# Softmax weights of later rows transposed on VectorE from blocks regrouped through DRAM, instead of on TensorE

## The chip, the cores and the metric

The kernel runs on one core of a Trainium2 chip. A core has a TensorE (PE) for matrix products, with the weight loads shown on their own as PEld; a VectorE (DVE), a ScalarE (ACT) and a GpSimd (POOL) for elementwise work; and SyncE (SP), which here only issues transfers. The engines run side by side and wait for each other through semaphores; each works through its own instructions in order. The metric is the time of one execution on the device in microseconds (us). All data is 32-bit floating point (f32).

## The reference

A block of cross-attention to a small bank of context rows, a mixture of three experts with soft routing, and a gate. B = 8 rows, T = 512 tokens, H = 256 channels, P = 64 context rows, E = 3 experts with RH = 512 hidden units.

```python
nx = _layer_norm(x, ln_gamma, ln_beta)
q = nx @ Wq
k = prototype_bank @ Wk
v = prototype_bank @ Wv
scores = jnp.einsum('bth,bph->btp', q, k) * H ** (-0.5)
weights = jax.nn.softmax(scores, axis=-1)
evidence = jnp.einsum('btp,bph->bth', weights, v)
anchor = jnp.broadcast_to(global_anchor[:, None, :], nx.shape)
combined = jnp.concatenate([nx, evidence, anchor], axis=-1)
router_probs = jax.nn.softmax(combined @ router_W + router_b, axis=-1)
h = jax.nn.silu(jnp.einsum('btc,ecr->bter', combined, e_w1) + e_b1)
expert_out = jnp.einsum('bter,erh->bteh', h, e_w2) + e_b2
routed = jnp.sum(expert_out * router_probs[..., None], axis=-2)
g = jax.nn.sigmoid(jax.nn.silu(combined @ gate_w1 + gate_b1) @ gate_w2 + gate_b2)
return x + g * (routed @ out_w + out_b)
```

## The kernel before

**Tiling.** The eight rows go in four pairs, j = 0 to 3. A pair's two rows are treated as a 2x2 block matrix, and the products are done with seven block products instead of eight; this is why differences of tiles are formed everywhere. Activations are held with channels on the 128 partitions and the 512 tokens along the free dimension (tiles of 128x512), the state in which TensorE wants them as the moving operand.

**Softmax weights.** `scores` computes the scores with *tokens* on the partitions: tile w of a pair is 128 partitions x 4 token groups x 2 rows x 64 context rows. `softmax` normalizes one row of the pair in it (L555, L556). The products of `evidence` need the same numbers the other way round: tile wT, 128 partitions (2 rows x 64 context rows) x 512 tokens. `transpose_w` makes it: four TensorE transposes of 128x128 into a PSUM bank (tile pt_w, L564) and a copy on ScalarE (L567). `evidence` multiplies it with vw, the value rows already multiplied by the first-layer weights (`value_weights`, L631, copied by L638, with a difference of two parts on VectorE at L645).

**Order.** The order on every engine is the order of the program: the lists `within` and `between` in the main loop put the small steps of a pair at named points of the large products. A pair runs `gate_layer`, three times `expert_layer`, then `outputs`. While `outputs` of pair j runs its second-layer products (12 matmul instructions for each 128x512 result, from L656), the steps in `between` prepare pair j + 1: scores, softmax, the transposes, the differences T on GpSimd (`combine_x`, L521), the value weights and the router. So there are three such blocks; in the profile they lie near 105 to 158, 213 to 266 and 321 to 374 us.

In `outputs` the points concerned come in this order: P2 (scores and softmax of the second row, differences of x), products, one output finished, P7 (`transpose_w`, value weights of expert 0, router logits), products, one output finished, P3 (value weights of expert 1, the router's exponentials), products, the last output finished, P4 (`router` for both rows). An output is finished by `finish`: L959 adds the PSUM result, L960 multiplies by the gate, L961 transposes the 32x32 blocks on VectorE, L962 adds x on GpSimd, and L951 stores it with four transfers on SP's queue. There are two buffers for yb, so every second output uses the same one.

`router` ends with the probabilities pr (L598, L600, L602 on VectorE, for each row). At the end of the next pair's gate products, `spread_probabilities` transposes the two pr on TensorE (tile pt_p, L615), copies them out (L616) and spreads them over all partitions through DRAM. Right behind pt_p come the first products of `evidence` with wT.

**Blocks through DRAM.** The normalized x of later pairs is already turned in this manner: `store_x` writes it to DRAM (xd, L497), `regroup_x` loads it back with `load_blocks` (L390) in such an order that each 32x32 block stands where its transpose belongs, and `transpose_blocks` (L509) lets VectorE transpose the blocks in place. All these transfers are on SP's queue. SP waits there for the write before it issues the loads.

PSUM has eight banks; small results take turns in the banks that `spares` names, through `misc`.

Of the kernel before, what the change touches and what calls it, by code (L numbers as in the profile page):

```python
# [8 lines left out]
F32 = mybir.dt.float32  # L9
# [7 lines left out]
def kernel(  # L17
# [50 lines left out]
    nc = tc.nc  # L68
    P = 128
    B, T, H = x.shape  # L70
    CT = context.shape[1]
    E, C3, RH = e_w1.shape
    KH = H // P
# [12 lines left out]
    dram = ctx.enter_context(tc.tile_pool(name="dram", bufs=2, space=bass.MemoryType.DRAM))  # L86
# [3 lines left out]
    work = ctx.enter_context(tc.tile_pool(name="work", bufs=2))  # L90
# [33 lines left out]
    def load_x(b):  # L124
        x_sb[b] = xpool.tile([P, NT, H], F32, tag="x", name=f"x_{b}")
        nc.sync.dma_start(x_sb[b], x[b].rearrange("(t p) d -> p t d", p=P))
# [5 lines left out]
    def rows_of(w):  # L132
        return w.rearrange("(k p) n -> p k n", p=P)
# [249 lines left out]
    def load_blocks(dst, src):  # L383

        for k in range(KH):
            for i in range(P // TB):
                lo = k * P + i * TB
                nc.sync.dma_start(  # L390
                    dst[i * TB : (i + 1) * TB, k, :].rearrange("r (j c) -> r j c", c=TB),
                    src[:, lo : lo + TB].rearrange("(j r) c -> r j c", r=TB),
                )
# [9 lines left out]
    def load_second(e):  # L403
        load_blocks(w2[e], e_w2[e])
# [44 lines left out]
    S = {}  # L449
# [102 lines left out]
    def softmax(b):  # L552
        w, sm = S["w", b // 2][:, :, b % 2, :], S.pop(("sm", b))
        rs = work.tile([P, NT], F32, tag="rs", name=f"rs_{b}")
        nc.vector.reciprocal(rs, sm)  # L555
        nc.vector.tensor_tensor(w, w, rs.unsqueeze(2).to_broadcast([P, NT, CT]), ALU.mult)  # L556

    def transpose_w(j):

        w = S["w", j]  # L560
        wT = work.tile([P, T], F32, tag="wT", name=f"wT_{j}", bufs=1)
        pt = misc(f"pt_w_{j}")
        for t in range(NT):
            nc.tensor.transpose(  # L564
                pt[:, t * P : (t + 1) * P], w[:, t, :, :].rearrange("p i c -> p (i c)"), ident
            )
        nc.scalar.copy(wT, pt)  # L567
        S["wT", j] = wT
# [487 lines left out]
    with tc.manual_schedule(engines=None):  # L1056
        ctx_rows = context.flatten_outer_dims().rearrange("(t p) d -> p t d", p=P)
        for d in range(2):
            half = slice(d * NX // 2, (d + 1) * NX // 2)
            nc.sync.dma_start(ctx_sb[:, half, :], ctx_rows[:, half, :])  # L1060
        nc.scalar.dma_start(wk_sb, rows_of(Wk))
        nc.scalar.dma_start(wv_sb, rows_of(Wv))
        load_x(0)
        nc.sync.dma_start(wq_sb, rows_of(Wq))
        load_x(1)
        for g in (E, 0):
            load_first(g)
            load_anchor(g)
        for g in (1, 2):
            load_first(g)  # L1070

        wake(7)
        context_transposes()
        project_keys()
        statistics(0, 0, NT)
        deviation(0, 0)
        normalize(0)
        project(wv_sb, ctxT, lambda m, ps: nc.scalar.copy(vT[:, m, :], ps), "v")
        small_transposes()
        wq_transposes()  # L1080
        transpose_x(0)
        router_anchor()
        statistics(1, 0, NT)
        deviation(0, 1)
        normalize(1)
        load_table(AF.Exp)
        project(wqT, kT, keep_m, "m")
        combine_weights(E)
        value_weights(0, E)
        spread_router_rows(0)  # L1090
        transpose_x(1)
        combine_x(0, nc.vector, (0, 1))
        scores(0)
        scores(1)
        load_table(AF.Silu)
        combine_weights(0)
        softmax(0)
        value_weights(0, 0, nc.vector.tensor_copy)
        anchor_rows(E)
        anchor_rows(0)  # L1100
        softmax(1)
        combine_x(0, nc.vector, (2, 3))
        combine_weights(1)
        combine_weights(2)
        late_scratch()
        load_anchor(1)
        load_anchor(2)
        nc.sync.dma_start(ow_sb, rows_of(out_w))
        nc.sync.dma_start(gw2_sb, rows_of(gate_w2))
        combine_gate()  # L1110
        load_second(0)

        for j in range(NP):


            within, between = {}, {}

            def put(where, n, step, *args):
                where.setdefault(n, []).append(lambda: step(*args))

            if j == 0:
                put(within, "gate", value_weights, 0, 1)
                put(within, (0, "A"), anchor_rows, 1)
                put(within, (0, "A"), router_logits, 0)
                put(within, (0, "A"), load_second, 1)
                put(within, (0, "B"), second_bias)
                put(within, (0, "B"), router_logits, 1)
                put(within, (0, "C"), transpose_second, 0)
                put(within, (0, "C"), anchor_columns, 1)
                put(within, (0, "C"), anchor_rows, 2)  # L1130
                for b in range(2):
                    put(within, (0, "C"), router_exp, b)
                    put(within, (0, "D"), router, b)
                put(within, (0, "C"), load_second, 2)
                put(within, (0, "D"), second_layer, 0)
                put(within, (0, "D"), spread_probabilities, 0)
                put(within, (0, "D"), combine_second, 0)
                put(within, (1, "A"), transpose_second, 1)
                put(within, (1, "B"), second_layer, 1)
                put(within, (1, "B"), combine_second, 1)  # L1140
                put(within, (1, "C"), transpose_second, 2)
                put(within, (1, "C"), anchor_columns, 2)
                put(within, (1, "D"), second_layer, 2)
                put(within, (1, "D"), combine_second, 2)
            if j:
                put(within, "gate end", spread_probabilities, j)
            put(within, (0, "C" if j == 0 else "B"), value_weights, j, 2)
            put(within, (1, "C"), load_x_blocks, 2 * j)
            put(within, (2, "A"), gate_differences, j)
            put(within, (2, "C"), load_x_blocks, 2 * j + 1)  # L1150
            if j + 1 < NP:
                b0, b1 = 2 * j + 2, 2 * j + 3
                put(within, "gate", load_x, b0)
                put(within, "gate", load_x, b1)
                put(within, (0, "A" if j else "D"), statistics, b0, 0, NT)
                put(within, (0, "C") if j else (1, "A"), statistics, b1, 0, NT)
                for i in range(2):
                    put(within, (1, "C"), deviation, j + 1, i)
                where = (1, "D") if j else (2, "B")
                put(within, where, normalize, b0)  # L1160
                put(within, where, store_x, b0)
                put(within, where, regroup_x, b0)
                put(within, (2, "C"), normalize, b1)
                put(within, (2, "C"), store_x, b1)
                put(between, "begin", transpose_blocks, b0)
                put(between, "gate", regroup_x, b1)
                put(between, "P1", scores, b0)
                put(between, "begin", value_weights, j + 1, E)
                put(between, "begin", spread_router_rows, j + 1)
                put(between, "P5", softmax, b0)  # L1170
                put(between, "P5", transpose_blocks, b1)
                put(between, "P6", router_logits, b0)
                put(between, "P2", scores, b1)
                put(between, "P2", softmax, b1)
                put(between, "P2", combine_x, j + 1, nc.gpsimd)
                put(between, "P7", transpose_w, j + 1)
                put(between, "P7", value_weights, j + 1, 0)
                put(between, "P7", router_logits, b1)
                put(between, "P3", value_weights, j + 1, 1)
                put(between, "P3", router_exp, b0)  # L1180
                put(between, "P3", router_exp, b1)
                put(between, "P4", router, b0)
                put(between, "P4", router, b1)
            gate_layer(j, within)
            for e in range(E):
                expert_layer(j, e, within)
            outputs(j, between)
# [34 lines left out]
```

## Time and profile before

| What | us |
|---|---|
| Median of 3 runs (475.64 to 476.08) | 476.01 |
| The profiled execution | 476.25 |
| Its span, first to last instruction | 474.5 |
| PE busy in the span | 469.6 |
| DVE busy in the span | 353.4 |
| L564, one of 16 transposes of w on PE | 0.273 |
| L567, one of 4 copies of wT on ACT | 0.587 |
| L509, one of 12 block transposes on DVE | 0.688 |

Times inside the profile count from the start of the span. The granted TensorE clock is 1.000. Busy time of PE is not time at its peak: matmuls overlap, and their ends are modelled, so starts of instructions are the safer measure. A line of the timeline gives start, duration, engine, line of the kernel, operation, output and input tiles, and in brackets the idle time of the engine ahead of it with what ended it.

### The profile page before, as it was taken

How to read it: one execution, taken by the hardware profiler on the slowest of the kernel's cores; microseconds unless marked ns; L12 is line 12 of the kernel's file. 1: busy time of each engine (PE TensorE's matmuls, PEld its weight loads, DVE VectorE, ACT ScalarE, POOL GpSimd, SP SyncE). 2: the span in 40 equal slices, each digit the busy share in tenths (PEclk: the TensorE clock that was granted, in tenths of full speed). 3: DMA queues.
4: the chain of work that ended last, by engine and by line, in shares of the span. 5: the costliest groups of instructions: out<-in, count | busy, mean ns of one | idle time of the engine just before them, and what ended most of it. 6: DMA issues, size and time to landing. Idle time of an engine off the chain costs nothing.

```text
span 474.5 us, 4652 instructions
## 1 busy us (share of the span) xinstructions
PE 469.6 (99%) x1451; PEld 225.1 (47%) x1451; DVE 353.4 (74%) x649; ACT 218.4 (46%) x391; POOL 78.2 (16%) x96
## 2 busy tenths in 40 slices
PE   9999999999999999999999999999999999999997
PEld 7654646435454444445454444445454444444454
DVE  2755766989989555889989565898989624697982
ACT  3555656557321546748320456758221365458000
POOL 5227032300062200000062200000042300000020
PEclk9999999999999999999999999999999999999999
DMA  8988330048311840342111750252011560000013
GB/s 285 369 126 159 59 134 1 0 103 104 33 22 22 168 145 0 78 101 44 17 24 22 155 155 2 62 115 46 18 22 22 83 185 0 1 0 1 0 22 67
DMA packets 118120, 35.27 MB, mean 74 GB/s; under 512 B 104732, under 2 KB 115088, under 8 KB 117584
## 3 DMA queue, kind: packets, MB, share of 16 engines
q1 hardware_dynamic: 114736, 27.02, 28.4%
q0 software_dynamic: 1472, 7.18, 4.7%
q10 hardware_dynamic: 1888, 0.79, 0.6%
q8 instruction: 11, 0.18, 0.2%
q14 instruction: 13, 0.11, 0.1%
HBM read 27.57 MB, written 7.40 MB: 74 GB/s over the span
## 4 chain that ended last, share of the span: by engine, by line
PE 94%; DVE 4%; issue 1%; ACT 0%; ACTq 0%
PE ps_u L656 42%; PE ps_z L656 18%; PE ps_y L656 15%; PE ps_vw L631 5%; PE ps_gu L656 3%; PE ps_s L531 3%; PE ps_w2o L416 2%; PE ps_gz L656 1%; DVE h L930 1%; PE ps_wake L255 1%; PE ps_k L310 1%; DVE h L739 1%; PE ps_gy L656 1%; PE ps_v L298 1%; PE ps_ar L354 0%
## 5 line engine op out<-in xcount | busy, mean ns | idle before, releaser
L739 DVE TENSOR_TENSOR h<-h,pb 128x512 f32<-128x512 f32 x96 | 61.9, 693 | 10.5 <-ACT h L689 10.5
L656 PE MATMUL ps_u<-h,w2o 128*128 128x512 f32 x144 | 63.9, 593 | 0.0
L656 PE MATMUL ps_u<-nxT,w 128*128 128x512 f32 x112 | 55.6, 607 | 0.0
L689 ACT ACTIVATE h<-h,abias 128x512 f32<-128x512 f32 x72 | 49.2, 718 | 8.7 <-DVE h L695 8.2
L656 PE MATMUL ps_z<-wT,vw 64*128 64x512 f32 x104 | 49.5, 605 | 0.0
L962 POOL TENSOR_TENSOR yb<-yb,xb 128x512 f32<-128x512 f32 x14 | 19.1, 1365 | 149.5 <-DVE yb L961 145.2
L656 PE MATMUL ps_z<-h,w2s 128*128 128x512 f32 x96 | 42.8, 595 | 0.2 <-DVE r L945 0.2
L698 ACT COPY h<-ps_u 128x512 f32<-128x512 f32 x48 | 28.0, 583 | 32.2 <-PE ps_u L656 31.9
L656 PEld LDWEIGHTS ps_u<-h,w2o 128*128 128x128 f32 x144 | 27.1, 190 | 31.3 <-issue 29.7
L695 DVE TENSOR_TENSOR h<-h,ps_y 128x512 f32<-128x512 f32 x24 | 16.4, 683 | 28.5 <-PE ps_y L656 28.5
L930 DVE TENSOR_TENSOR h<-h,h 128x1024 f32<-128x1024 f32 x24 | 34.3, 1483 | 0.0
L656 PEld LDWEIGHTS ps_u<-nxT,w 128*128 128x128 f32 x112 | 19.9, 189 | 29.7 <-issue 22.8
L689 ACT ACTIVATE h<-ps_u,abias 128x512 f32<-128x512 f32 x24 | 16.5, 687 | 30.4 <-PE ps_z L656 30.4
L656 PE MATMUL ps_y<-nxT,w 128*128 128x512 f32 x56 | 28.6, 592 | 0.0
L656 PE MATMUL ps_z<-T,ws 128*128 128x512 f32 x56 | 28.6, 592 | 0.0
L656 PEld LDWEIGHTS ps_z<-h,w2s 128*128 128x128 f32 x96 | 17.9, 190 | 22.1 <-issue 21.1
L656 PE MATMUL ps_u<-wT,vw 64*128 64x512 f32 x56 | 27.8, 611 | 0.0
L656 PE MATMUL ps_y<-wT,vw 64*128 64x512 f32 x56 | 27.0, 596 | 0.0
L631 PE MATMUL ps_vw<-w,vT 128*128 128x512 f32 (+1 forms) x64 | 26.9, 541 | 0.0
L656 PE MATMUL ps_u<-T,ws 128*128 128x512 f32 x56 | 26.7, 594 | 0.0
L656 PE MATMUL ps_u<-T,w 128*128 128x512 f32 x56 | 26.6, 592 | 0.0
L656 PE MATMUL ps_z<-nxT,ws 128*128 128x512 f32 x56 | 26.6, 592 | 0.0
(206 smaller groups left out, 771.8 us busy)
## 6 DMA issues: line engine op xcount, KB each, us to landing
pb<-pd POOLq DMA_DIRECT2D x4, 1536.0 KB, 7.1
x<-in_x_dram SPq DMA_DIRECT2D x8, 512.0 KB, 5.9
xb<-in_x_dram SPq DMA_DIRECT2D x64, 64.0 KB, 2.5
out_dram<-yb SPq DMA_DIRECT2D x56, 64.0 KB, 2.0
w<-in_L_xcond_e_w_dram SPq DMA_DIRECT2D x6, 512.0 KB, 9.3
xd<-x SPq DMA_DIRECT2D x6, 512.0 KB, 3.0
xg<-xd SPq DMA_DIRECT2D x48, 64.0 KB, 2.4
scr_wa<-in_L_xcond_e_w_dram SPq DMA_DIRECT2D x3, 512.0 KB, 4.7
```

The costliest lines, as they stand in the source:

```text
L255: nc.tensor.matmul(ps_wake[0][:, :P], zeros, zeros, start=True, stop=True)
L298: nc.tensor.matmul(ps, w_sb[:, k, m * P : (m + 1) * P], src[:, k, :], start=(k == 0), stop=(k == KH - 1))
L416: nc.tensor.matmul(ps[:, d * H : (d + 1) * H], w2T[:, k, (i + d) * P : (i + d + 1) * P], ow_sb[:, k, :], start=(k == 0), stop=(k == KH - 1),)
L531: nc.tensor.matmul(ps[:, t, :], nxT[:, k, t * P : (t + 1) * P], mr[:, k, b, :], start=(k == 0), stop=(k == KH - 1),)
L631: nc.tensor.matmul(ps, vT[:, k, j * 2 * CT : (j + 1) * 2 * CT], w1[:, KH + k, n0:n1], start=(k == 0), stop=(k == KH - 1),)
L656: nc.tensor.matmul(ps, lhsT, rhs, start=start, stop=True, skip_group_check=not start)
L689: nc.scalar.activation(h, h if src is None else src, AF.Silu, bias=abias[:, c, 2 * j + i : 2 * j + i + 1])
L695: nc.vector.tensor_tensor(h, h, part, ALU.add)
L698: nc.scalar.copy(chunk(n, i, d), part)
L739: nc.vector.tensor_tensor(h, h, S["pb", j][:, i, 2 * q // RC, :], ALU.mult)
L930: nc.vector.tensor_tensor(d, p, m, ALU.subtract)
L962: nc.gpsimd.tensor_tensor(yb, yb, S["xb", 2 * j + row][:, i, :], ALU.add)
```

## The change

For the pairs j = 1 to 3, `transpose_w` (four TensorE transposes and a ScalarE copy) is replaced by two steps. `regroup_w`, at P2 behind the softmax, writes w to DRAM (tile wd, 256 KB) and loads it back in blocks of 32x32 into a new tile wg with four transfers of 64 KB, all on SP's queue. `transpose_w_blocks`, at P3 behind the value weights of expert 1, has VectorE transpose all blocks with one instruction into wT. `load_blocks` takes the number of its groups of 128 columns from the tile it fills, so that it serves both uses. Pair 0 keeps `transpose_w`.

```diff
-        for k in range(KH):
+        for k in range(dst.shape[1]):
             for i in range(P // TB):
                 lo = k * P + i * TB
                 nc.sync.dma_start(
...
+    def regroup_w(j):
+
+        wd = dram.tile([T, P], F32, tag="wd", name=f"wd_{j}")
+        nc.sync.dma_start(
+            wd.rearrange("(t p) c -> p t c", p=P), S["w", j].rearrange("p t i c -> p t (i c)")
+        )
+        S["wg", j] = work.tile([P, 1, T], F32, tag="wg", name=f"wg_{j}", bufs=1)
+        load_blocks(S["wg", j], wd)
+
+    def transpose_w_blocks(j):
+        S["wT", j] = work.tile([P, T], F32, tag="wT", name=f"wT_{j}", bufs=1)
+        nc.vector.transpose(S["wT", j], S.pop(("wg", j))[:, 0, :])
...
                 put(between, "P2", softmax, b1)
+                put(between, "P2", regroup_w, j + 1)
                 put(between, "P2", combine_x, j + 1, nc.gpsimd)
-                put(between, "P7", transpose_w, j + 1)
                 put(between, "P7", value_weights, j + 1, 0)
                 put(between, "P7", router_logits, b1)
                 put(between, "P3", value_weights, j + 1, 1)
+                put(between, "P3", transpose_w_blocks, j + 1)
                 put(between, "P3", router_exp, b0)
```

## The prediction

> **What bounds the kernel now.** I read the page first (busy shares, then the chain that ended last), then the chain in the window 340 to 380 us, then the timelines of DVE, POOL and the PE weight loads there, and last the DMA issues. Page and chain:
>
> ```profile
> PE 469.6 (99%) x1451; PEld 225.1 (47%) x1451; DVE 353.4 (74%) x649; ACT 218.4 (46%) x391; POOL 78.2 (16%) x96
> ...
> PE 94%; DVE 4%; issue 1%; ACT 0%; ACTq 0%
> ```
> ```profile
> 349.27 5.20 PE ps_u L656 x12
> 354.47 0.48 PE pt_w L564 x4
> 354.95 1.72 PE ps_vw L631 x4
> ```
>
> PE is the path: whatever leaves PE shortens the span, unless another engine then holds it. The four transposes of the softmax weights stand on the path with 0.48 us. Next, DVE, POOL and the weight loads at the end of the same block (start us, duration us):
>
> ```profile
> 367.67 0.71 DVE L961 STREAM_TRANSPOSE yb<-r 128x512 f32<-128x512 f32 x1
> 368.41 0.42 DVE L645 TENSOR_TENSOR vw<-vw 64x256 f32<-64x256 f32 x1
> 368.86 0.69 DVE L959 TENSOR_TENSOR r<-r,ps_u 128x512 f32<-128x512 f32 x1
> 369.59 0.93 DVE L960 TENSOR_TENSOR r<-r,hg 128x512 f32<-128x512 f32 x1
> 370.61 0.71 DVE L961 STREAM_TRANSPOSE yb<-r 128x512 f32<-128x512 f32 x1
> ...
> 371.61 1.09 DVE L602 TENSOR_TENSOR pr<-ex,rrs 128x12 f32<-128x12 f32 x1
> ...
> 373.02 0.18 DVE L602 TENSOR_TENSOR pr<-ex,rrs 128x12 f32<-128x12 f32 x1
> ```
> ```profile
> 368.46 1.50 POOL L962 TENSOR_TENSOR yb<-yb,xb 128x512 f32<-128x512 f32 x1 [5.08 <-DVE yb L961]
> 371.40 1.27 POOL L962 TENSOR_TENSOR yb<-yb,xb 128x512 f32<-128x512 f32 x1 [1.44 <-DVE rsm L598]
> ```
> ```profile
> 373.39 0.09 PEld L615 LDWEIGHTS pt_p<-ident,pr 128*12 128x12 f32 x1 [0.24 <-DVE pr L602]
> 373.82 0.09 PEld L615 LDWEIGHTS pt_p<-ident,pr 128*12 128x12 f32 x1 [0.34 <-issue]
> ```
>
> No DVE line carries an idle time: from 352.83 us, where L555 had waited for ACT's exponentials, to 373.20 us (373.02 + 0.18) DVE works without a gap. Its last product is pr of the second row, and PE loads that as weights (pt_p) at 373.82. A finished DVE instruction frees a PE load about 0.12 us later: L556 ended at 354.17 (353.04 + 1.13), the load for pt_w began at 354.29. So pr is ready for PE at 373.32, and DVE has only 0.50 us of room before PE waits. The same rows of the other two blocks: pr ends at 156.64 and 264.92, the load begins at 157.32 and 265.57, room 0.56 and 0.53 us. PE is nominally the bound, but at the end of each of the three blocks DVE is half a microsecond behind it.
>
> **What the Trainium skill says.** "VectorE: DVE Perf Modes", section "The three transpose paths", has VectorE's transpose work on blocks of 32x32 alone and write to SBUF, TensorE's on the whole 128x128 into PSUM. The code before already follows this: L509 transposes regrouped blocks in 688 ns, and pt_w needs a copy out of PSUM (L567, 587 ns). "GPSIMD Engine Reference", section "Key points": GpSimd shares its SBUF interfaces with VectorE, and contends with DVE instructions in a 2-port mode or with two SBUF inputs. The trace agrees: the product L602 of 12 elements takes 1.09 us beside POOL's L962 and 0.18 without; L960 takes 0.93 instead of 0.69. A transpose has one input and needs about a cycle an element, so it should be free of this, and the trace shows it: these two transposes start in the middle of POOL's subtractions (the next one follows at 77.85 and takes 0.73 too) and take no longer than the pair at 67.94, where POOL is idle (1.30 us as well).
>
> ```profile
> 77.17 0.73 POOL L204 TENSOR_TENSOR w2o<-w2o 128x256 f32<-128x256 f32 x1
> ```
> ```profile
> 77.40 1.30 DVE L408 STREAM_TRANSPOSE scr_w2T<-scr_w2T 128x512 f32<-128x512 f32 x2
> ```
>
> **Part by part**, for one of the three blocks, with the times of the third.
>
> *Removed from PE:* four transposes. L631 now starts at 354.79; the 12 products before it began at 349.11, and 12 that follow score matmuls take 5.20 us (331.87 to 337.07 in the same block), so L631 could start at 354.31: gain 0.48. Blocks one and two: 138.28 - 132.64 - 5.20 = 0.44, 246.53 - 240.86 - 5.20 = 0.47. Sum 1.39 us. The wait of pt_w for DVE's L556 goes too, but it was hidden: the products streamed until then.
>
> *Removed from ACT:* the copy L567, 0.59 us. Nothing: ACT then sits idle for 1.13 us until the next copy, and no one waits for that one (its reader L645 comes 5 us later).
>
> *PSUM rotation:* with pt_w gone, the two ps_vw tiles take banks 6 and 7 instead of 7 and 4. Bank 6 was last used at the block's start, bank 7 by the first scores. Nothing; if a bank were still being read, PE would stall before L631.
>
> *Added on SP's queue,* between the four stores of the first output and those of the second: one write wd (256 KB) and four loads wg (64 KB each).
>
> ```profile
> 351.34 23.30 SPq L951 DMA_DIRECT2D out_dram<-yb  x16
> ```
> ```profile
> xd<-x SPq DMA_DIRECT2D x6, 512.0 KB, 3.0
> xg<-xd SPq DMA_DIRECT2D x48, 64.0 KB, 2.4
> ```
>
> The first four stores are issued by about 353.4 (0.52 us each). wd waits for L556, 354.2; it lands within 3.0 us like xd, twice as large: 357.2. The loads wait on SP for that, are issued at 0.52 us each until 359.3, and land 2.4 us later: 361.7. The transpose takes its place on DVE at 368.86, 7.1 us later. SP is kept by this until 359.3; the next stores wait for POOL's sum, which ends at 363.38 (361.88 + 1.50), so they lose nothing. "DMA: Bandwidth & Descriptors", section "Anatomy of one DMA — SWDGE (gpsimd) path", puts about 2.0 us of fixed cost on a transfer that GpSimd issues, mostly the receipt; the 3.0 and 2.4 of the trace for SP's transfers are in line with it. If the round trip took over 14.7 us, DVE and then PE would stand still for the rest.
>
> *Added on DVE:* one transpose of 128x512, right behind L645, in the gapless stretch. It starts when L959 does now, 368.86. Its four DMA waits are handled while L645 runs (as before L509, which starts with no gap). Two transposes in a row take 1.30 us with 0.69 each, so one delays the next instruction by 0.61: L959 at 369.47. L960 follows 0.73 later, 370.20. By then POOL's sum (368.46 + 1.50 = 369.96) is over, so L960 takes 0.69 instead of 0.93: the delay falls to 0.37. L961, POOL's last sum and both L602 move with it by 0.37. Bounds of this delay, which no row shows: below 0.18 if another collision with POOL also goes away (nothing else in the stretch has one that could: L602 follows the sum that L961 starts, and moves with it); above 0.86, if the transpose takes the 0.71 of L961, three of its waits at 50 ns each are exposed and L960 gains nothing. I take 0.37, because each term is read from a row.
>
> *Moved:* what waits behind the transpose on DVE is the last output (L959 to L961), then both pr; for pr waits PE, for the last output POOL and SP. The stores and then the loads of x for the next pair go out 0.37 later: x leaves SP at 158.14 and lands in 5.9 us, 164.0; DVE reads it at 165.68. Covered by 1.6 us.
>
> *Sum.* PE reaches the pt_p load at 373.82 - 0.48 = 373.34; pr is ready at 373.20 + 0.37 + 0.12 = 373.69. PE waits 0.35, and of the gain 0.13 is left (room 0.50 less delay 0.37). Blocks one and two: 0.56 - 0.37 = 0.19, 0.53 - 0.37 = 0.16. Together 0.48 us. Behind this point DVE waits for PE again (0.82 us at 374.02), so nothing is carried into the next pair. Within each block DVE meets PE for the last time near 337 us, well ahead of the removed transposes, so no earlier start of DVE comes out of them. Profiled execution: 476.25 (span 474.5) - 0.48 = 475.77; it lay 0.24 above the median, so against the median 476.01 I expect about 475.5.
>
> **Rivals.** A measurement of this kernel can't tell changes under 0.2%, 0.95 us, from none.
> A. *DVE gives no hold:* the whole 1.39 us comes, 474.6. For it: the chain has pt_w wholly on PE. Against: needs a delay of pr under 0.05 us, and no row gives that back.
> B. *The slower side: the delay of pr is the upper bound.* In each block pr comes 0.86 us later, 0.30, 0.33 and 0.36 beyond the room: +1.0, 477.0. It decides as soon as the delay passes the room, about 0.53 us; visible from 0.85 on. For it: L961 with its six waits starts 0.10 us after the instruction before it ends. Against: L960's collision ends at a POOL time that the change doesn't move.
> C. *The transpose is held by POOL* until 369.83, where L960 really starts today (369.59 + 0.93 - 0.69): pr 1.36 later, 0.83 beyond the room in each, +2.5, 478.5; a late regroup looks the same. Against: the overlap at 77.40, and 7.1 us of cover.
> That the swap doesn't happen can be left out: the diff takes transpose_w out of the three later pairs and leaves nothing in its place but the new steps.
>
> **How the numbers follow.** Forecast 0.60, A 0.15, B 0.17, C 0.08. Predicted: 475.5. Leaving out C and the outer halves of A and B (about 0.2) puts the ends of the range at A's 474.6 and just over B's 477.0. Faster by over 0.2%: most of A and the forecast's edge, 0.16. Slower: C and over half of B, 0.19. Within: 0.65.
>
> **What would show it.** Right: L564 x4 instead of x16, three transposes wT of about 0.69 us with no DMA wait, L960 behind them 0.69 instead of 0.93, and the pt_p load idle for some 0.35 us longer than now, put down to DVE's pr. Wrong: no idle time there (A); L960 still at 0.93, or the transpose starting well after L645's end (B); a transpose over 1 us or with a DMA as its releaser (C).

## The result and the profile after

| | Median, us | Profiled execution | Span |
|---|---|---|---|
| Before | 476.01 (13 runs, 475.55 to 476.44) | 476.25 | 474.5 |
| Changed | 474.71 (13 runs, 474.47 to 475.19) | 475.19 | 473.4 |

The changed kernel takes 0.9975 of the time before, with a 95% interval of 0.9968 to 0.9982; the medians differ by 1.3 us. That is inside the forecast range and about 0.8 us below the forecast of 475.5.

In the page of the changed kernel the engines' busy times and the chain that ended last look like those shown of before:

```profile
PE 468.2 (99%) x1439; PEld 223.9 (47%) x1439; DVE 354.8 (75%) x652; ACT 216.5 (46%) x388; POOL 78.2 (17%) x96
...
PE 93%; DVE 4%; DMA 1%; issue 1%; ACT 0%; ACTq 0%
```

PE has 12 instructions and 1.4 us less, DVE three instructions and 1.4 us more: the transposes have moved. The chain in the third block, where pt_w stood between the products and the value weights:

```profile
349.95 3.86 PE ps_u L669 x9
353.82 1.72 PE ps_vw L644 x4
```

Nothing is left between them. The end of this block on DVE (lines moved by 13: L961 is now L974, L645 L658, L959 L972, L960 L973, L602 L615):

```profile
367.00 0.71 DVE L974 STREAM_TRANSPOSE yb<-r 128x512 f32<-128x512 f32 x1
367.75 0.42 DVE L658 TENSOR_TENSOR vw<-vw 64x256 f32<-64x256 f32 x1
368.20 0.71 DVE L569 STREAM_TRANSPOSE wT<-wg 128x512 f32<-128x512 f32 x1
368.84 0.65 DVE L972 TENSOR_TENSOR r<-r,ps_u 128x512 f32<-128x512 f32 x1
369.52 0.69 DVE L973 TENSOR_TENSOR r<-r,hg 128x512 f32<-128x512 f32 x1
...
372.71 0.18 DVE L615 TENSOR_TENSOR pr<-ex,rrs 128x12 f32<-128x12 f32 x1
```

and the weight loads of PE there, with the first product of evidence behind them:

```profile
372.45 0.09 PEld L628 LDWEIGHTS pt_p<-ident,pr 128*12 128x12 f32 x1 [0.43 <-DVE pr L615]
372.94 0.09 PEld L628 LDWEIGHTS pt_p<-ident,pr 128*12 128x12 f32 x1 [0.41 <-DVE pr L615]
373.15 0.18 PEld L669 LDWEIGHTS ps_y<-wT,vw 64*128 64x128 f32 x1
```

The transpose starts at once behind L658, without a wait for a transfer, and L973 now takes 0.69 instead of 0.93, since POOL's sum (367.80 + 1.51 = 369.31) is over when it starts. From the start of L658 to the end of the second pr it was 4.79 us (368.41 to 373.20) and is 5.14 us (367.75 to 372.89): pr comes 0.35 later. Both pt_p loads now wait for pr. PE is held by DVE here, as forecast, but for less time.

**A ruler for small changes.** The start of the program differs between executions by more than half a microsecond: the first product of evidence starts between 35.33 and 36.08 us in the traces of all these runs. So I read the gain of each block as the change in the distance from the last group of products of evidence of the first pair (it starts at 99.54 us before and 99.59 after, ahead of everything that the change touches) to the first product of evidence behind each block:

| Start of that product | Block 1 | Block 2 | Block 3 |
|---|---|---|---|
| Before | 157.63 | 265.88 | 374.13 |
| Changed | 157.30 | 265.22 | 373.15 |
| Gain of the block (with the 0.05 later start) | 0.38 | 0.33 | 0.32 |

Sum 1.03 us, where the removal alone should give 1.39. The experiments ask where the other 0.36 goes, and why it isn't the 0.91 of the forecast.

### The profile page after: what moved, and what is told of

Same layout as the page of the kernel before. It is cut to its first block, busy times and chain, and to the rows that moved or that the text cites. A ratio compares the mean times of both kernels' runs of the same rounds, so it can differ in the third digit from the quotient of the medians.

```text
span 473.4 us, 4652 instructions
## 1 busy us (share of the span) xinstructions
PE 468.2 (99%) x1439; PEld 223.9 (47%) x1439; DVE 354.8 (75%) x652; ACT 216.5 (46%) x388; POOL 78.2 (17%) x96
## 4 chain that ended last, share of the span: by engine, by line
PE 93%; DVE 4%; DMA 1%; issue 1%; ACT 0%; ACTq 0%
PE ps_u L669 42%; PE ps_z L669 18%; PE ps_y L669 15%; PE ps_vw L644 5%; PE ps_gu L669 3%; PE ps_s L531 3%; PE ps_w2o L416 2%; PE ps_gz L669 1%; DVE h L943 1%; DMA scr_ctx<-in_ctx_dram 1%; DVE h L752 1%; PE ps_k L310 1%; PE ps_v L298 1%; PE ps_gy L669 1%; PE ps_ar L354 0%
## 5 line engine op out<-in xcount | busy, mean ns | idle before, releaser
L644 PE MATMUL ps_vw<-w,vT 128*128 128x512 f32 (+1 forms) x64 | 26.9, 541 | 0.0
```

Source lines behind the costliest of these rows:

```text
L644: nc.tensor.matmul(ps, vT[:, k, j * 2 * CT : (j + 1) * 2 * CT], w1[:, KH + k, n0:n1], start=(k == 0), stop=(k == KH - 1),)
```

## The experiments

Theories. **HOLD:** PE waits at pt_p for pr, and every bit by which pr comes later than the room allows is lost on PE. **FREE:** PE isn't held, the missing part is start and noise. **TRANSFERS:** the added transfers take it. Each run was timed beside the kernel before on the same chip, and the last column is the difference to that median; "block gains" are read with the ruler above from one trace of each run.

| Run | Block gains, us | Sum | Median less that of before |
|---|---|---|---|
| Changed kernel, again beside the second run of "router first" | 0.38, 0.33, 0.32 | 1.03 | -1.18 |
| Without the transpose | 0.43, 0.48, 0.47 | 1.38 | -1.37 |
| Transpose twice | -0.38, -0.41, -0.42 | -1.21 | +1.40 |
| Before + one spare transpose | 0.00, 0.01, 0.00 | 0.01 | +0.08 |
| Before + two spare transposes | -0.36, -0.41, -0.40 | -1.17 | +1.48 |
| Before + transfers alone | 0.00, 0.01, 0.00 | 0.01 | 0.00 |
| Transpose ahead of L658 | -0.20, -0.26, -0.25 | -0.71 | +0.66 |
| Router first | 0.44, 0.47, 0.48 | 1.39 | -1.58, -1.50 |
| Before + router first | 0.00, 0.00, -0.01 | -0.01 | 0.00 |
| Regroup late | -2.51, -2.84, -4.63 | -9.98 | +12.77 |

### The transpose taken away, and made twice

```diff
-        S["wT", j] = work.tile([P, T], F32, tag="wT", name=f"wT_{j}", bufs=1)
-        nc.vector.transpose(S["wT", j], S.pop(("wg", j))[:, 0, :])
+        S["wT", j] = S.pop(("wg", j))[:, 0, :]
```

> The changed kernel without VectorE's transpose of wg: the products of evidence read wg as it is, so the part that puts the 32x32 blocks right is left out. Theory HOLD (at the end of each block PE waits for the second pr, which the added transpose delays by about 0.35 us; that eats 0.36 of the 1.39 us that the removed PE transposes give): about 0.36 us below the changed kernel, 474.35, and the second pt_p weight load no longer waits for DVE. Rival FREE (PE isn't held, the rest of the gain is lost in the start of the program and in noise): 474.7, the same pt_p gap as in the changed kernel. Rival TRANSFERS (the missing part goes to the added transfers): 474.7.

Measured: 474.42, ratio 0.9971 (0.996 to 0.9983), block gains that sum to 1.38. PEld in its third block:

```profile
371.32 0.09 PEld L627 LDWEIGHTS pt_p<-ident,pr 128*12 128x12 f32 x1 [0.24 <-DVE rsm L610]
371.75 0.09 PEld L627 LDWEIGHTS pt_p<-ident,pr 128*12 128x12 f32 x1 [0.34 <-DVE pr L614]
```

The idle times are those of before, 0.24 and 0.34: PE's own pace. pr ended at 371.58, 0.17 ahead of the second load. All regroup transfers are still made here. So the 0.36 us is the cost of the transpose on DVE, and not of the transfers. The median alone could not tell this from the changed kernel (the intervals overlap); the block gains do.

The reverse, two transposes of wg into the same wT:

```diff
+        wg = S.pop(("wg", j))[:, 0, :]
+        nc.vector.transpose(S["wT", j], wg)
-        nc.vector.transpose(S["wT", j], S.pop(("wg", j))[:, 0, :])
+        nc.vector.transpose(S["wT", j], wg)
```

> The changed kernel with VectorE's transpose of wg made twice into the same tile. HOLD: pr comes another 0.61 us later (pitch of two transposes) and PE waits for all of it: 3 x 0.61 = 1.8 above the changed kernel, 476.5. FREE: under 0.3 more, at most 475.0. TRANSFERS: 474.7.

Measured: 477.19, ratio 1.0029 (1.0019 to 1.0039), slower than before. DVE in the third block:

```profile
369.40 0.71 DVE L570 STREAM_TRANSPOSE wT<-wg 128x512 f32<-128x512 f32 x1
370.15 0.71 DVE L571 STREAM_TRANSPOSE wT<-wg 128x512 f32<-128x512 f32 x1
370.79 0.65 DVE L974 TENSOR_TENSOR r<-r,ps_u 128x512 f32<-128x512 f32 x1
```

The second transpose costs 0.75, not 0.61: it starts 0.75 after the first, while L974 starts 0.64 after the second (370.79 - 370.15). It writes the tile that the first one writes and reads the same input; which of these keeps the two from overlapping was not tested. pr is 1.10 late (5.89 from L660's start at 368.95, instead of 4.79), and the blocks lose 0.38 to 0.42. FREE falls: at most 475.0 was its number.

### How much room there is: spare transposes in the kernel before

```diff
+    def spare_turns(j):
+        wx = work.tile([P, T], F32, tag="wx", name=f"wx_{j}", bufs=1)
+        for _ in range(1):
+            nc.vector.transpose(wx, S["w", j].rearrange("p t i c -> p (t i c)"))
...
                 put(between, "P3", value_weights, j + 1, 1)
+                put(between, "P3", spare_turns, j + 1)
```

> The kernel before, TensorE's transposes kept, with one spare VectorE transpose of w into an unused tile where the change puts its own. HOLD: pr comes 0.37 us later, inside the room of before (0.67 to 0.73 us by the two traces, 0.50 to 0.56 by the prediction): no change, 476.0.

Measured: 475.81, ratio 1.0 (0.9992 to 1.0008). One transpose of 0.71 us on DVE, no transfer, nothing taken from PE: no block moves by more than 0.01 us. With `range(2)`:

> The kernel before with two such spare transposes. pr comes 0.98 us later. Room 0.67 to 0.73: 0.25 to 0.31 beyond it in each block, +0.84, 476.85. Room 0.50 to 0.56 as the prediction had it: +1.35, 477.35. FREE: 476.0.

Measured: 477.21, ratio 1.0028 (1.0017 to 1.004). Again the second transpose costs 0.75, so pr is 1.08 late in block 3 (368.96 to 374.83). With the room of 0.67 to 0.73 that makes 0.35 to 0.41 in each block, 1.14 together, with the room of 0.50 to 0.56 it makes 1.65. The blocks show 0.36, 0.41 and 0.40, 1.17 together, so the larger room is right. My figure of 0.84 was too low because it took 0.61 for the second transpose. The run with one spare transpose fits both rooms and cannot tell them apart.

### The transfers alone

The kernel before, with `regroup_w` added at P2 and nothing that reads wg; TensorE's transposes kept.

```diff
                 put(between, "P2", softmax, b1)
+                put(between, "P2", regroup_w, j + 1)
```

> The kernel before with the regroup through DRAM added (one write, four loads in each block, into a tile that nothing reads), TensorE's transposes kept. HOLD: no change, 476.0. TRANSFERS: 0.3 to 0.4 more, 476.35.

Measured: 475.73 beside 475.73, ratio 1.0 (0.9992 to 1.0009), no block moves by more than 0.01. TRANSFERS falls. In the changed kernel SP's queue shows them in the third block, with the stores of the second output behind them at the moment when POOL's sum is ready:

```profile
350.69 1.95 SPq L964 DMA_DIRECT2D out_dram<-yb  x4
353.58 0.38 SPq L561 DMA_DIRECT2D wd<-w  x1
355.95 1.91 SPq L390 DMA_DIRECT2D wg<-wd  x4
362.74 11.59 SPq L964 DMA_DIRECT2D out_dram<-yb  x12
```

The last load was issued by 357.86 and these loads land in 2.3 us (median), about 360.2; the transpose starts at 368.20, eight microseconds later.

### The place of the transpose on DVE

```diff
-                put(between, "P3", value_weights, j + 1, 1)
                 put(between, "P3", transpose_w_blocks, j + 1)
+                put(between, "P3", value_weights, j + 1, 1)
```

> The changed kernel with the transpose one place earlier on DVE, ahead of the difference of vw (L658) instead of behind it. HOLD with the shared SBUF interface: L658 with its two inputs now falls into POOL's sum and waits for its end, about 1 us; pr comes about 1.2 us later than before the change (0.35 now), 0.5 beyond the room in each block: about 477.5. If the place doesn't matter: 474.7.

Measured: 476.45, ratio 1.0014 (1.0007 to 1.002). DVE and POOL in the third block:

```profile
368.12 0.67 DVE L569 STREAM_TRANSPOSE wT<-wg 128x512 f32<-128x512 f32 x1
368.82 1.00 DVE L658 TENSOR_TENSOR vw<-vw 64x256 f32<-64x256 f32 x1
369.86 0.69 DVE L972 TENSOR_TENSOR r<-r,ps_u 128x512 f32<-128x512 f32 x1
```
```profile
368.28 1.27 POOL L975 TENSOR_TENSOR yb<-yb,xb 128x512 f32<-128x512 f32 x1 [5.08 <-DVE yb L974]
```

The mechanism is as expected: the same two instructions in the other order, and L658, with two inputs, stands in POOL's sum and takes 1.00 instead of 0.42, while the transpose beside POOL takes 0.67. The size was too high: 1.5 us were expected, about half of it came. One reason is that POOL's sum takes 1.27 here instead of 1.50. It starts beside the transpose; the sums of the changed kernel that start while L658 runs take 1.50 (361.21) and 1.51 (367.80), the one that starts later 1.26 (371.09). pr is 0.93 late (373.95 - 367.49 from the start of L974, against 373.20 - 367.67 of before), which leaves 0.20, 0.23 and 0.26 beyond the room: 0.69, measured 0.71. One place earlier on DVE would have turned the gain into a loss.

### Taking the hold away

The probabilities move ahead of the last output's finish. The finish then fills time in which DVE waits anyway.

```diff
             experts(u, lambda q: a(q, 1, 1), 0, 1)
+            run("P4")
             finish(r21, u, 1, 0)
-            run("P4")
```

> The changed kernel with the router's probabilities (point P4) put ahead of the last output's finish, so that pr is ready about 2 us before PE needs it and the finish fills DVE's idle time behind it. HOLD: the hold goes, 0.36 below the changed kernel, 474.35; the product L615 of the first pr no longer meets POOL's sum (0.18 instead of 1.09 us). FREE: 474.7. A loss would mean that the later finish holds the gate sums of the next pair.

Measured: 474.21, ratio 0.9967 (0.9954 to 0.9979). The second run beside the changed kernel, on one chip:

> The changed kernel once more, on the same chip as the next run: 1.0 to 1.3 us below the kernel before.

> The changed kernel with the router's probabilities ahead of the last output's finish, once more beside the changed kernel itself. HOLD: 0.36 below it, and 1.4 below the kernel before. FREE: equal to the changed kernel.

Measured: 474.71 for the changed kernel (0.9975, 0.9966 to 0.9984), 474.39 for this one (0.9969, 0.9957 to 0.998). DVE in the third block, from the first of the two runs:

```profile
367.35 0.71 DVE L569 STREAM_TRANSPOSE wT<-wg 128x512 f32<-128x512 f32 x1
...
368.35 0.18 DVE L615 TENSOR_TENSOR pr<-ex,rrs 128x12 f32<-128x12 f32 x1
...
368.84 0.18 DVE L615 TENSOR_TENSOR pr<-ex,rrs 128x12 f32<-128x12 f32 x1
...
372.04 0.69 DVE L708 TENSOR_TENSOR hg<-hg,ps_u 128x512 f32<-128x512 f32 x1 [0.90 <-PE ps_u L669]
```

pr is ready at 369.02, 2.8 us before the load that needs it (371.84); its first product no longer meets POOL (0.18 instead of 1.08); DVE waits for PE again behind it. The block gains are 0.44, 0.47 and 0.48: the whole of what leaves PE. The difference of 0.3 us to the changed kernel is inside the intervals of the medians; it rests on the blocks, which repeat to 0.01 us in both traces of the changed kernel. The same edit on the kernel before:

> The kernel before with the router's probabilities put ahead of the last output's finish. HOLD: pr isn't late in the kernel before, so nothing comes of it: 476.0 within 0.15. If it gains as much as the same edit does on the changed kernel, the hold isn't the reason of that gain.

Measured: 475.73 beside 475.73, ratio 1.0001 (0.9993 to 1.0009). It gains nothing where pr isn't late, so what it gives on the changed kernel is the hold.

### The regroup issued too late

```diff
-                put(between, "P2", regroup_w, j + 1)
...
+                put(between, "P7", regroup_w, j + 1)
                 put(between, "P7", value_weights, j + 1, 0)
```

> The changed kernel with the regroup issued one point later (P7), so that its write stands on SP's queue behind the stores of the second output, which wait for POOL's sum until 363.4 (times of the third block before). Write at 365.4, landed 368; loads issued until 370, landed 372.3; the transpose, due at 368.9, waits 3.4 us, and with it pr. HOLD: each block 3.4 + 0.35 - 0.70 beyond the room, about +9 on the kernel before, 485. If only wT itself mattered (ready at 373.1, needed at 373.65): 474.7.

Measured: 488.66, ratio 1.0275 (1.026 to 1.0291). DVE and PE in the third block:

```profile
378.96 0.71 DVE L569 STREAM_TRANSPOSE wT<-wg 128x512 f32<-128x512 f32 x1 [3.33 <-DMA wg<-wd]
```
```profile
383.20 0.28 PE L628 MATMUL pt_p<-ident,pr 128*12 128x128 f32 x1 [2.90 <-DVE pr L615]
```

The transpose waits 3.33 us (3.4 expected), and PE waits for pr, not for wT, which was ready at 379.67. pr is 3.64 late in this block, which less the room of 0.67 makes 2.97 (3.1 expected). The total is 3.8 us above the expected 9. The trace accounts for 11.4 us: the waits cost 2.51, 2.84 and 3.08, somewhat less than expected, and a slower PE behind the waits of blocks 2 and 3 costs about 3.0, told in the last section. The median lies another 1.2 us above the profiled execution (487.45). The three other executions ran at a granted clock of 0.989 to 0.990 against its 0.993, so more time at a slower PE would fit; it is not shown.

## Why the prediction was right, and where it was off

- **Removed from PE** (0.44, 0.47, 0.48 forecast): L644 starts at 137.90, 245.73 and 353.65. Against before, and less what the earlier blocks had already gained, this is 0.43, 0.47 and 0.48. Right, and shown by the two runs without a hold, which gain 1.38 and 1.39.
- **Delay of pr** (0.37): 0.36, 0.37 and 0.35, with the pitch of 0.64 instead of 0.61 and L973's release as forecast. Right.
- **Transfers, ACT, PSUM banks, next pair** (nothing): right for the transfers by the run with them alone; for the others, the runs without a hold gain all of the 1.39 us, so nothing else took a part of it.
- **PE held at pt_p by pr:** right, shown by taking the transpose away, by doubling it, and by taking the hold away.
- **The room** (0.56, 0.53, 0.50 in the order of the blocks) is the term that was mis-sized. I measured it to the start of the second pt_p load, with 0.12 us from pr to the load. But in the kernel before, that load (373.82) starts with the first pt_p matmul, at PE's own pace, and the first product of evidence follows 0.31 us later. PE in the third block, before and changed:

```profile
373.82 0.38 PE L615 MATMUL pt_p<-ident,pr 128*12 128x128 f32 x2
374.13 0.69 PE L656 MATMUL ps_y<-wT,vw 64*128 64x512 f32 x1
```
```profile
372.69 0.53 PE L628 MATMUL pt_p<-ident,pr 128*12 128x128 f32 x2
373.15 0.69 PE L669 MATMUL ps_y<-wT,vw 64*128 64x512 f32 x1
```

  When PE really waits, the load starts 0.05 after pr's end (372.94 - 372.89), and the product 0.21 after the load: 0.26 from pr to the product, the same in all three blocks of the changed kernel and where the transpose runs twice or ahead. Measured to that product the room of before is 157.63 - 156.64 - 0.26 = 0.73, then 0.70 and 0.67. Less the delay, that gives 0.37, 0.33 and 0.32; the trace has 0.38, 0.33 and 0.32. The forecast lost 0.17 us in each block (0.07 from pr to the load, 0.10 from the load to the product), 0.51 in all, and that is nearly all of the difference between 0.48 and the 1.03 of the trace.
- **The range** held the result because its lower end stood at A's 474.6, not because the forecast's sum was right: 0.48 us is less than half of what the blocks gained.
- **The rivals:** the median, 1.30 us below before, is nearer to A (the whole 1.39) than to the forecast, but A's mechanism is wrong: PE is held. B's price came in where the delay passed the room (two transposes, or the earlier place). C's first half, a transpose held by POOL, doesn't happen: in the changed kernel it starts at 368.20, inside POOL's sum (367.80 to 369.31), and takes 0.71 us. Its second half, a late regroup, happens once the transfers are put a point later.
- **The size of the sum:** 1.03 us by the blocks, 1.06 by the spans, 1.30 and 1.18 by the medians. The spans differ from the blocks by the 0.05 later start and by 0.08 at the end of the program: from the start of the last product of evidence to the end of the span it is 48.83 us before, 48.75 in the changed kernel and 48.71 with the transfers alone. The interval of the ratio, 0.9 to 1.5 us, holds all of these; what of the rest is the execution's start stays open.

The version with the router first is faster than before by 1.5 to 1.6 us, and by its blocks 0.36 faster than the changed kernel.

## What to carry to other kernels

When work moves from the bounding engine to another, look for the last thing that the bounding engine waits for in that stretch, and count the room up to the first instruction that really can't start without it, not to a wait whose start the engine's own queue had set. If the other engine is gapless there, order matters as well as length: what nobody waits for (an output's finish) belongs behind what the bounding engine waits for (pr), and a two-input instruction belongs outside GpSimd's sums (L658 took 1.00 us instead of 0.42 inside one). The round trip through DRAM cost nothing here as long as its issue wasn't queued behind a store that waited for something late.

## What the runs showed that I had not expected

In the late-regroup run PE idles at the end of each block. After an idle time of 2.40 us (block 1) the products go on at their normal pitch of 0.43 us. After 2.67 us (block 2: 267.67 to 270.34) and 2.90 us (block 3) the pitch is 0.86, and the granted clock from 385 to 387 us is 0.52. PE in the third block:

```profile
385.02 1.06 PE L669 MATMUL ps_y<-wT,vw 64*128 64x512 f32 x1
...
385.88 1.06 PE L669 MATMUL ps_y<-wT,vw 64*128 64x512 f32 x1
...
387.25 0.59 PE L669 MATMUL ps_u<-wT,vw 64*128 64x512 f32 x1
```

The normal pitch is back at 387.25. From the first product of evidence to the first one for ps_u it takes 1.82 in the kernel before (374.13 to 375.95, the first ps_u product), 3.24 here (384.01 to 387.25): 1.4 us lost beyond the wait itself, 1.55 in block 2 (271.13 to 274.50). "TensorE: Matmul & The Clock Gate" of the Trainium skill, section "Part 1: The HAM clock gate", gives half the clock after an idle window of about 3.4 us. The idle times here are shorter, but they don't show that less is enough. The granted clock is still 1.00 up to 270.8 and 383.5, when the first pt_p matmul (270.34, 383.20) has already run, and is at or near 0.50 from 270.9 and from 383.5 on. That is 3.2 us after the end of the last full product (267.67 and 380.30), with at most the two small pt_p matmuls in between. From there to the next full product it is 3.46 and 3.71 us in blocks 2 and 3, but 3.09 in block 1 (156.95 to 160.04), where the clock stays at 1.00. So the trace agrees with the page if the two small matmuls don't end the idle window; no run here tests that. What the trace does show is that a hold can cost more than its length: the two longer ones here cost 1.4 to 1.55 us more.
